# One more half-size product cut into quarters in each projection, and where its operand sums are placed

## The chip, the cores and the metric

The kernel runs on one core of a Trainium2 chip. The metric is device time in microseconds; the median of three runs is shown, and one further execution was taken by the hardware profiler. TensorE (PE) multiplies; VectorE (DVE) and ScalarE (ACT) read its results out of PSUM; GpSimd (POOL) adds and subtracts in SBUF; SyncE (SP) issues the DMAs.

## The reference

Two layers over 64 batches of 256 tokens by 512 features, all float32:

```python
# layer 0
h = relu(layernorm(x))
x = x + (adj @ h) @ W0 + b0
# layer 1: attention with 8 heads of 64, masked by adj
h = relu(layernorm(x))
q, k, v = (h @ Wq + bq), (h @ Wk + bk), (h @ Wv + bv)
attn = softmax(q @ k.T / 8 + (1 - adj) * -1e9)      # per batch and head
x = x + (attn @ v) @ Wo + bo
```

The projections q, k, v and o (512 features to 512 features) are what the change touches.

## The kernel before

**Groups and stages.** Two batches make a group, so there are 32 groups. Layer 0 fills the first 650 us or so and leaves its results in DRAM. The attention stage then works group by group; each group has two attention halves (`qd` 0 and 1, four heads each). From group `FIRST2 = 2` on, a cycle of the stage is: `attend(g, 0)` (denominators `pden` and the product with v, `pav`), `score(g, 1)`, then the query and key projections of group g+1 in the order `QK`, then `attend(g, 1)`, `score(g+1, 0)`, then the value projection of group g+1 interleaved with the output projection of group g in the order `VO`. The last group uses the orders `V1`, `O1` and `OL` instead.

**Seven products for eight.** A projection multiplies a 2 by 2 arrangement of weight blocks by a 2 by 2 arrangement of activation blocks, with seven products in the manner of Strassen and Winograd. The names are in `BLOCKS`: A is a11 b11, B is s3 t3, C is a12 b21, D is a22 t4, E is s4 b22, F is s2 t2, G is s1 t1. The `s` are sums of weight blocks, made once; the `t` are differences of activation blocks, made for each group (class `Halves`): t1 = b12 - b11, t3 = b22 - b12 (written over b12), t2 = b22 - t1, t4 = b21 - t2. One such product at full size is four matmuls of 128x128 by 256 columns (`product`).

**Quarter size.** `SMALL` names the products that are cut once more in the same way: seven matmuls of 128x128 by 128 columns in place of four of 256. They need the same seven combinations one level down: weight sums from `block_sums` (once, early in the stage) and activation sums from `Blocks.sums` (each group, on POOL), called by `block_hidden` for q, k and v and by `block_outputs` for o. Before, q, k and v have C to G at quarter size and o has C, D and E; A and B (and o's F and G) are at full size.

**How a quarter-size product gets out of PSUM.** `sums` multiplies the first four of the seven into a small bank: a running total and, beside it, a rest. Between two multiplications the total is read out. In `added` (C, D, E) ACT or DVE put these parts into the result; in `staged` (F, G) ACT copies them to SBUF, DVE adds the rest and later adds everything into the bank. The last three multiplications go straight into a bank (`last_three`).

**The order of work.** `QK`, `VO`, `V1`, `O1` and `OL` are written-out orders. In the token `qGf`, q is the projection, G the product, f its step; `kp00`, `qm11` and the like put or add a bank into one quarter of the result; `x` takes the next exponent (`next_exponent`, an ACT instruction at L1122); `|` is one tick of a clock. Work put down with `after(n, ...)` is issued n ticks later. Every engine works through what was issued to it in that order.

**POOL's queue around this.** In the value half: the inversion of the denominators (`invert`, L1163 to L1165: one multiply, one scale, one multiply, after an ACT logarithm and exponential), the subtraction of the row maximum for two of the score's four parts (L1108, the other two are done by DVE alone), the sums of the output operand (`t_o`, L481, and `block_outputs`, L578 to L580), the key sums (`key_sum`, L1129, four additions that `pden` needs), the hidden sums of the next group (`t_h`). In the query-key half: the rest of the hidden sums and `block_hidden`, then the inversion, the two subtractions, one sum of `t_o`, the key sums. `score` seeds two pairs of banks on ACT first and then runs what waits in the list `behind_seeds`, which is the inversion; after that come the score's matmuls and their evacuation.

**Buffers.** Denominators and their inverse (`den`, `rden`) lie in a tile called `rest`, which also holds the o sums of C and E. Key sums lie in the tile `as`, one buffer, rewritten in every half. Quarter-size sums of q, k and v lie in a tile `t2` and in a part of `spare`, those of o's D in `t24o`. Spare room for weight sums and these is taken from tiles of layer 0 that are no longer in use.

Of the kernel before, what the change touches and what calls it, by code (L numbers as in the profile page):

```python
# [8 lines left out]
F32 = mybir.dt.float32  # L9
# [48 lines left out]
def general_path(tc, x, adj, w0, b0, wq, bq, wk, bk, wv, bv, wo, bo, out):  # L58
# [154 lines left out]
V1 = (
    "vFa vA0 vFb vA1 vFc vFd x vA2 | vA3 vGa vFe vEa vp00 vCa vFf vGb | vB0 vEb vFg vCb vFi x vGc vFh vFj vFk vGd "
    "vFl | vEc vGe vEd vCc vEe vCd vp10 vGf vEf2 vDa vCe vGg vB1 vCf | vEf vDb vB2 x vGh vGi vGj vEg vGl vB3 | "
    "vCg vp11 vDc vCh vDd vGk x vDe vCi vDf vCj vDi vm11 | vDj vDk vCk vm10 vDg vEi vEj vCl vEk | vDh vEl0 vEl1 "
    "vEl2 vEh ")
# [11 lines left out]
def kernel(  # L229
# [314 lines left out]
    SMALL = {"q": "CDEFG", "k": "CDEFG", "v": "CDEFG", "o": "CDE"}  # L544
# [3 lines left out]
    def block_sums(n):  # L548

        todo = []  # L550
        for x in SMALL[n]:
            w = W[n][BLOCKS[x][0]]
            def part(i, j):
                return w[:, j, i * P:(i + 1) * P]
            s1, s2, s4 = (spare.pop(0) for _ in range(3))
            W2[n, x] = dict(a11=part(0, 0), a12=part(0, 1), a22=part(1, 1), s1=s1, s2=s2, s3=part(1, 0), s4=s4)
            eng = nc.vector if x in "FG" else nc.gpsimd
            for o, p, q, op in ((s1, part(1, 0), part(1, 1), ALU.add), (s2, s1, part(0, 0), ALU.subtract),
                                (part(1, 0), part(0, 0), part(1, 0), ALU.subtract), (s4, part(0, 1), s2, ALU.subtract)):
                todo.append((eng.tensor_tensor, o, p, q, op))  # L560
        return todo

    class Blocks:
# [7 lines left out]
        def operand(self, n):  # L571
            if n[0] == "t":
                return self.t[..., {"t1": 0, "t3": 1, "t2": 2, "t4": 3}[n], :]
            return self.x[..., int(n[1]) - 1, int(n[2]) - 1, :]

        def sums(self, eng):
            t, op = self.t, ALU.subtract
            eng.tensor_tensor(t[..., 0:2, :], self.x[..., :, 1, :], self.x[..., 0, :, :], op=op)  # L578
            eng.tensor_tensor(t[..., 2, :], self.operand("b22"), t[..., 0, :], op=op)
            eng.tensor_tensor(t[..., 3, :], self.operand("b21"), t[..., 2, :], op=op)  # L580

    def quartered(g, n, halves, blocks, by_token, place, first, seeds=None, multiplied=None, done=None):
# [102 lines left out]

        def added(x, to, quadrant=None, begin=False):
# [36 lines left out]
        product("B", "pc", True)  # L723
# [346 lines left out]
    A, AS, behind_seeds, exponents = {}, {}, [], []  # L1070

    def score(g, qd, sum_delay=5, exps=(3, 4, 5, 8)):
# [10 lines left out]
        for c in range(2):  # L1083
            for b in range(GB):
# [46 lines left out]
    def attend(g, qd):  # L1131
# [19 lines left out]
        if i == 0:  # L1151
            AS["rest"] = act.tile([P, 4, GN], F32, tag="yT1", name="rest")
        den, rden = AS["rest"][:, 0, :], AS["rest"][:, 1, :]
# [16 lines left out]
        else:  # L1170
            behind_seeds.append(invert)
# [98 lines left out]
    for g in range(NG):  # L1270
# [106 lines left out]
```

## Time and profile before

| what | us |
|---|---|
| median of 3 runs | 2641.59 |
| lowest and highest run | 2637.54, 2641.89 |
| profiled execution: its own time | 2640.46 |
| profiled execution: span from first to last instruction | 2638.1 |
| layer 0, before the first `pden` | 660.0 |
| one cycle of the steady stretch (two halves) | 62.0 |

The profile is of one execution. A group of instructions is given by line, engine, operation, names of what it writes and reads, shapes and count; then its busy time in us, the mean ns of one, and the idle time of its engine just before it. A float32 matmul shows as two records. A timeline line gives the start and the length in us; x2 or x4 at its end says that so many equal records were merged. The names in lines of the trace are the program's: `q_pc` is q's bank pc, `k_Fs` the small bank of k's product F.

### The profile page before, as it was taken

What the parts mean: (1) busy time and instruction counts of PE and PEld (TensorE: products, weight loads), DVE (VectorE), ACT (ScalarE), POOL (GpSimd) and SP (SyncE); (2) the same over time, 40 slices, a digit from 0 to 9 for tenths busy, and PEclk for the clock granted to TensorE, in tenths of its full rate; (3) what the DMA queues carried; (4) which work ended last, traced back from release to release, by engine and by line L of the source; (5) the groups of instructions that cost most, each with busy time, mean ns of one, the idle gap of its engine ahead of it and who ended that gap; (6) DMA issues with size and microseconds to landing.
All of it is one profiled execution on the core that took longest, in us unless ns stands there. A gap on an engine that the chain in (4) does not pass through costs nothing. (4 is left out here: it accounts for less than half of the span.)

```text
span 2638.1 us, 54578 instructions
## 1 busy us (share of the span) xinstructions
PE 2599.2 (99%) x21156; PEld 2291.1 (87%) x21156; DVE 1835.3 (70%) x3999; ACT 1292.5 (49%) x2742; POOL 1948.3 (74%) x1897
## 2 busy tenths in 40 slices
PE   7999999999999999999999999999999999999997
PEld 6999899998788888888888888888888888888886
DVE  5878788875466666666666666666666666666666
ACT  3444454543444545555555455544454555555542
POOL 5888887773777777777777777777777777777774
PEclk9999999999999999999999999999999999999999
DMA  5776667664111222111111111111122221111101
GB/s 131 200 197 183 173 166 184 166 167 100 33 49 49 64 62 66 52 49 49 49 49 49 49 49 49 49 49 49 49 65 63 61 56 49 49 49 49 49 33 49
DMA packets 281077, 211.20 MB, mean 80 GB/s; under 512 B 145904, under 2 KB 212976, under 8 KB 280816
## 3 DMA queue, kind: packets, MB, share of 16 engines
q1 hardware_dynamic: 280352, 207.15, 30.0%
q8 instruction: 169, 2.77, 0.4%
q14 instruction: 92, 0.75, 0.1%
q10 hardware_dynamic: 464, 0.52, 0.1%
HBM read 106.96 MB, written 100.66 MB: 79 GB/s over the span
## 5 line engine op out<-in xcount | busy, mean ns | idle before, releaser
L1163 POOL TENSOR_TENSOR rest<-rest 128x512 f32<-128x512 f32 x63 | 80.2, 1273 | 425.0 <-ACT rest L1162 425.0
L1098 DVE SCALAR_TENSOR_TENSOR a<-sc,top 128x512 f32<-128x512 f32 x256 | 159.0, 683 | 278.0 <-PE sc L1090 277.9
L1108 POOL TENSOR_TENSOR a<-a,top 128x1024 f32<-128x1024 f32 x125 | 293.2, 2369 | 47.5 <-DVE a L1101 47.5
L1129 POOL TENSOR_TENSOR as<-a 128x512 f32<-128x512 f32 x256 | 318.3, 1275 | 5.8 <-ACT a L1122 5.8
L1122 ACT ACTIVATE a<-a 128x1024 f32<-128x1024 f32 x256 | 271.8, 1063 | 0.6 <-POOL a L1108 0.5
L1090 PE MATMUL sc<-q,k 64*128 64x256 f32 x2048 | 240.0, 383 | 1.4 <-ACT sc L289 1.4
L1090 PEld LDWEIGHTS sc<-q,k 64*128 64x128 f32 x2048 | 196.6, 186 | 45.5 <-ACT rest L1161 25.5
L1145 PE MATMUL pav<-a,v 128*32 128x256 f32 x4096 | 235.0, 381 | 0.0
L1145 PEld LDWEIGHTS pav<-a,v 128*32 128x32 f32 x4096 | 133.8, 111 | 89.2 <-issue 2.0
L1154 ACT ACTIVATE rest<-pden 128x512 f32<-128x512 f32 x64 | 38.2, 597 | 340.7 <-PE pden L1138 340.7
L42 DVE BATCH_NORM_STATS2 st<-x 128x6 f32<-128x512 f32 x256 | 173.1, 676 | 8.8 <-DMA x<-in_x_dram 6.6
L1101 DVE SCALAR_TENSOR_TENSOR a<-sc,maskT 128x512 f32<-128x512 f32 x256 | 158.1, 678 | 0.0
L289 ACT ACTIVATE sc<-maskT 128x512 f32<-128x512 f32 x256 | 137.5, 591 | 0.0
L800 ACT ACTIVATE h<-x,nb,rs 128x512 f32<-128x512 f32 x128 | 93.9, 803 | 75.3 <-POOL nb L54 75.3
L927 ACT ACTIVATE h<-x,nb,rs 128x512 f32<-128x512 f32 x128 | 97.2, 808 | 52.0 <-POOL nb L54 47.1
L645 PE MATMUL o_pa<-wo_s,t_o 128*128 128x256 f32 x480 | 118.8, 380 | 0.0
L772 DVE TENSOR_TENSOR x<-o_pa,x 128x512 f32<-128x512 f32 x120 | 82.5, 687 | 50.4 <-PE o_pa L645 50.4
L1183 DVE TENSOR_TENSOR oT<-pav,rest 128x512 f32<-128x512 f32 x128 | 82.0, 681 | 29.3 <-POOL rest L1165 29.3
L1016 ACT ACTIVATE k<-k_pa,bk_c 128x256 f32<-128x256 f32 (+1 forms) x150 | 61.3, 449 | 78.4 <-PE k_pa L631 78.1
L861 POOL TENSOR_TENSOR hs<-h 128x512 f32<-128x512 f32 x31 | 39.3, 1269 | 73.8 <-ACT h L800 63.7
L645 PEld LDWEIGHTS o_pa<-wo_s,t_o 128*128 128x128 f32 x480 | 84.3, 191 | 7.8
L1030 ACT COPY v<-v_pa 128x512 f32<-128x512 f32 (+1 forms) x90 | 42.8, 475 | 97.2 <-PE v_pa L631 95.6
(1644 smaller groups left out, 8238.7 us busy)
## 6 DMA issues: line engine op xcount, KB each, us to landing
x<-in_x_dram SPq DMA_DIRECT2D x256, 128.0 KB, 3.1
residual<-x SPq DMA_DIRECT2D x256, 128.0 KB, 2.5
hidden<-r SPq DMA_DIRECT2D x128, 256.0 KB, 4.5
h1T<-hidden SPq DMA_DIRECT2D x64, 512.0 KB, 7.4
x<-residual SPq DMA_DIRECT2D x32, 1024.0 KB, 7.5
out_dram<-x SPq DMA_DIRECT2D x62, 512.0 KB, 4.1
w_sb<-in_L_gnn_weight_dram SPq DMA_DIRECT2D x1, 1024.0 KB, 9.5
wq_sb<-in_L_gnn_Wq_dram SPq DMA_DIRECT2D x1, 1024.0 KB, 8.2
```

Source lines behind the costliest of these rows:

```text
L42: nc.vector.bn_stats(st, src)
L289: nc.scalar.mul(t, seed, times)
L645: nc.tensor.matmul(t[:, m, :], lhs, rhs, start=starts, stop=True, skip_group_check=True)
L800: nc.scalar.activation(H0[g][:, t, :], xt[:, t, :], AF.Relu, bias=nb[:, t % n:t % n + 1], scale=rs[:, t % n:t % n + 1])
L927: nc.scalar.activation(h1[:, k * NT + t, :], xt[:, k * NT + t, :], AF.Relu, bias=nb[:, t:t + 1], scale=rs[:, t:t + 1])
L1090: nc.tensor.matmul(ps[j][:, kt * N:(kt + 1) * N], k[j * HD:(j + 1) * HD, c, kt * P:(kt + 1) * P], q[j * HD:(j + 1) * HD, c, :], start=(kt ...
L1098: nc.vector.scalar_tensor_tensor(o, ps[j].rearrange("p (k n) -> p k n", k=NT), SCALE, top_b[:, 0:NT, :], op0=ALU.mult, op1=ALU.subtract)
L1101: nc.vector.scalar_tensor_tensor(o.rearrange("p k n -> p (k n)"), ps[j], SCALE, maskT_f, op0=ALU.mult, op1=ALU.add)
L1108: nc.gpsimd.tensor_tensor(a, a, top_b, op=ALU.subtract)
L1122: nc.scalar.activation(a, a, AF.Exp)
L1129: nc.gpsimd.tensor_tensor(AS[c, b], a4[:, :, 0, :], a4[:, :, 1, :], op=ALU.add)
L1145: nc.tensor.matmul(po[f][h * 32:(h + 1) * 32, b * N:(b + 1) * N], v[:, k, h * HD + f * 32:h * HD + f * 32 + 32], A[h // 2, b][:, (h % 2) * ...
```

## The change

1. `SMALL` gets B (s3 t3) for q, k and v, and F (s2 t2) for o. B's first four multiplications are a new function, `chain`: ACT copies the running total straight into bank pc (steps c, e, g), the rest goes to SBUF (n) and DVE adds it into pc at the end (k). The block sums of B's weights are put on DVE.
2. `Blocks.sums` makes four separate subtractions, with t3 written over b12, so a set of sums takes three blocks of room and not four.
3. `block_hidden` keeps only the sums of t1, t2 and t4's blocks (D, F, G) at its old place. The sums of b21's blocks (C) go to `behind_seeds`, after the inversion, which is put first in that list. The sums of t3's blocks (B, new) and of b22's (E) go to a new list, `behind_scores`, that `score` runs when it is through.
4. `block_outputs` makes the sums of t2's and t4's blocks first, then those of b21 and b22.
5. `den` and `rden` lie in the first half of the key sums' tile `as`; the room of `rest`, `t2` and `t24o` becomes fixed tiles for the sums (`KEPT`) and spare blocks.
6. All five orders are written anew.

The core of the diff (of the orders, QK in full and most of VO):

```diff
 QK = (
-    "kFa kCi kFb kCj kCk qFa kFc qFb kFd x qB0 | qGa qFc qFd kFe qA0 qFe x qA1 | qFf kFf qA2 qFg kFg qA3 qFh | "
-    "kA0 kFh qp000 kA1 qp001 kDa kA2 x qFl kA3 | qCi qGb qCj kp000 qCk qFi kp001 qCl qFj qFk | qGc kFl qp100 qGd "
-    "qDa qp101 kCl kB0 qGe kB1 qDb x qGi | qGf kFi qGg kCa kFj kCb kFk qGh qGj kp100 qGk | kCc kp101 qGl kCd kGa "
-    "qDc kCe kGb qDd kCf kGi kGc qDe | qDf kGd kCg kDb kGe kB2 kCh kGf kDc kGg qDg | kB3 qDh kDd kGh kp110 qCa "
-    "kDe qEa kp111 kDf qB1 qEb qCb qB2 | kGl kDi kDj kDk kDg km10 qEc qEd | qCc kDh qEe qCd kEa qEf qCe qB3 qCf "
-    "kEb kGj qEf2 qp110 kGk | kEc qp111 km11 kEd qEg kEe qCg qm11 qDi kEf qDj qDk qCh | kEi kEf2 kEj qm10 qEi qEj "
-    "kEg qEk kEk qEl1 | qEl2 kEl0 kEl1 qEl0 kEh qEh kEl2 ")
+    "qFa kA0 qFb kA1 kFa qFc x qCa | kA2 kA3 kFb qGa kp000 qFd kFc | kp001 kFd qA0 qFe kFe qA1 x qFf kFf | qA2 "
+    "qFg kFg qA3 qFh kFi kFh qp000 kFj kFk qp001 | qCi kFl qCj x kCa qCk qCb qFi kCb qFj qCl qGb qCc kp100 qCd | "
+    "qFl kCc kp101 kCd kGa x qCe qGc kCe qGd kCf kGi qCf kGj | qGe kGk kGb qFk kCg qp100 qGf kCh kGc qp101 qCg "
+    "kGd | qGg qCh kBa kGe kBb qGh qGi kBc qGj kGf qGl qDa kGg kBd | qBa qDb kBe qBb kGh kBn qGk qBc qDc kGl qDd "
+    "kBf qDe qBd | qDf kBg kCi kCj qBn kCk qBe kBh kCl kBi qDg qBf | qDh qEa qBg kEa kBj qEb kDa kEb kBk qBh qBi "
+    "kDb qBj kp110 | kEc qBk kp111 qEc qEd kDc qp110 km11 kDd qp111 kDi kEd kDe qEf | kDj kDf kEf kDk qm11 kEi "
+    "qEe kEj kEe qDi qEf2 kEk km10 kDg kEl0 | qEi kEf2 qDj kDh qDk qEg kEl1 qEj qm10 qEk kEg qEl0 | kEl2 kEh qEh "
+    "qEl1 qEl2 ")
 VO = (
...
-    "vEb vGi vGh x vGj vEc vGl vEd vDc vEe vDd | vEf vDj vDe vDk vDf vGk oA0 vm10 oA1 vm11 | vDg oA2 vEf2 vDh oA3 "
-    "vEi op00 vEj vEk | vEg vEl0 oCi oCa vEh oF0 oCb oF1 vEl1 vEl2 | oF2 oF3 oCc op10 oCd oEa oDa | oCe oB1 oCf "
-    "oB2 oDb oEb oB3 oDc | op11 oDd oEc oEd oDe oG0 oDf oDi oEe oG1 oEf | oG2 oG3 oCg om11 oDj oDk | oDg oCh oCj "
...
+    "vA0 oAz vA1 oBz vA2 vA3 x | vFa vCi vCj vCk vFb vp00 vBa vBb vFc x | vFd vGa vCl vFi vFj vFe vFk vBc vCa vGb "
+    "vFf | vCb vBd vFg vGc vGd vBe vCc vFh vGe vCd vFl x oA0 oEa | vCe vGf vCf vBf vp10 oEb oA1 vGg vCg vBn oA2 "
+    "vGh vBg | oA3 vCh x vGl oB0 vBh op00 oFa vBi | oFb vBj vDa vBk vEa vGi vDb vEb vGj vp11 vGk vEc | vDc vm11 "
+    "vEd vDd vEe vDi vEf vDe vDj vDf vDk vEi vEf2 vEj | vm10 vEk vDg vEl0 vEg vDh oFc oFd vEl1 oFi vEh oFe oFj | "
+    "vEl2 oFk oDa oFf oCa oFg oB1 oCb oB2 oFh | oFl oEc oEd oCc op10 oCd oB3 oCe oCi | oCf oCj op11 oG0 oG1 oDb "
+    "oEe oG2 oEf | oG3 oDc om11 oDd oCg oDi oDe oDj oDf | oDk oEi oCh oCk om10 oDg oEj oEk oDh oEg oCl0 | oEh "
+    "oCl1 oEl ")
...
-    SMALL = {"q": "CDEFG", "k": "CDEFG", "v": "CDEFG", "o": "CDE"}
+    SMALL = {"q": "BCDEFG", "k": "BCDEFG", "v": "BCDEFG", "o": "CDEF"}
...
-            eng = nc.vector if x in "FG" else nc.gpsimd
+            eng = nc.vector if x in "BFG" else nc.gpsimd
...
         def operand(self, n):
+            if n == "t3":
+                n = "b12"
             if n[0] == "t":
-                return self.t[..., {"t1": 0, "t3": 1, "t2": 2, "t4": 3}[n], :]
+                return self.t[..., {"t1": 0, "t2": 1, "t4": 2}[n], :]
             return self.x[..., int(n[1]) - 1, int(n[2]) - 1, :]
 
         def sums(self, eng):
-            t, op = self.t, ALU.subtract
-            eng.tensor_tensor(t[..., 0:2, :], self.x[..., :, 1, :], self.x[..., 0, :, :], op=op)
-            eng.tensor_tensor(t[..., 2, :], self.operand("b22"), t[..., 0, :], op=op)
-            eng.tensor_tensor(t[..., 3, :], self.operand("b21"), t[..., 2, :], op=op)
+            for o, p, q in (("t1", "b12", "b11"), ("t3", "b22", "b12"), ("t2", "b22", "t1"), ("t4", "b21", "t2")):
+                eng.tensor_tensor(self.operand(o), self.operand(p), self.operand(q), op=ALU.subtract)
...
+        def chain(x, b):
+
+            t, total, rest = sums(x, "adbf")
+            held = {}
+
+            def copy(name, i, k):
+                def todo():
+                    o = part(take(b, full=True), i, k)
+                    nc.scalar.copy(o, like(o, total()))
+                step(x + name, todo, t, b)
+
+            def keep_rest():
+                held[0] = act.tile([P, 2, 2, P], F32, tag="stage", name=f"{n}_{g}_{x}", bufs=2)[:, 0, 0:1, :]
+                nc.scalar.copy(held[0], rest())
+
+            def add_rest():
+                o = part(banks[b], 1, None)
+                add(o, o, like(o, held[0]))
+            copy("c", 0, 0)
+            step(x + "n", keep_rest, t)
+            copy("e", 1, 0)
+            copy("g", None, 1)
+            last_three(x, "hij", b)
+            step(x + "k", add_rest, b)
+
...
-        product("B", "pc", True)
+        if "B" in SMALL[n]:
+            chain("B", "pc")
+        else:
+            product("B", "pc", True)
...
-    kept = []
+    KEPT = {}
 
     def block_hidden(g, step):
 
-        t = act.tile([P, GB, 4, P], F32, tag="t2", name=f"t2_{g}")
-        both = Blocks(H1T[g][:, :, 2:4, :].rearrange("p k c (n j) -> p k c n j", j=P), t)
-        last = Blocks(HH[g].all.rearrange("p t c (n j) -> p t c n j", j=P), kept[0])
-        after(step, both.sums, nc.gpsimd)
+        x = H1T[g]
+        both = Blocks(x[:, :, 2:4, :].rearrange("p k c (n j) -> p k c n j", j=P), KEPT["h2"])
+        third = Blocks(x[:, 1, 0:2, :].rearrange("p c (n j) -> p c n j", j=P), KEPT["h3"][:, 3])
+        last = Blocks(HH[g].all.rearrange("p t c (n j) -> p t c n j", j=P), KEPT["h3"][:, 0:3])
         after(step, last.sums, nc.gpsimd)
-        H2[g] = {"C": both.one(0), "E": both.one(1), "G": last.one(0), "F": last.one(1), "D": last.one(2)}
+        behind_seeds.append(lambda: both.one(0).sums(nc.gpsimd))
+        behind_scores.append(lambda: third.sums(nc.gpsimd))
+        behind_scores.append(lambda: both.one(1).sums(nc.gpsimd))
+        H2[g] = {"C": both.one(0), "E": both.one(1), "G": last.one(0), "F": last.one(1), "D": last.one(2), "B": third}
 
     def block_outputs(g, step):
         x = OT[g][:, 2:4, :].rearrange("p c (k n j) -> p k c n j", k=GB, j=P)
-        if g < NG - 1:
-            t4 = act.tile([P, 4, P], F32, tag="t24o", name=f"t24o_{g}")
-            t = AS["rest"][:, 2:4, :].rearrange("p k (q j) -> p k q j", j=P)
-        else:
-            t4 = kept[0][:, 0]
-            t = act.tile([P, GB, 4, P], F32, tag="t2", name=f"t2o_{g}")
-        both = Blocks(x, t)
-        last = Blocks(HO[g].t["t4"].rearrange("p c (n j) -> p c n j", j=P), t4)
+        t = KEPT["o" if g < NG - 1 else "h3"]
+        both = Blocks(x, t[:, 0:2])
+        last = Blocks(HO[g].all[:, 1:3].rearrange("p t c (n j) -> p t c n j", j=P), t[:, 2:4])
         if g == NG - 1:
             both.sums(nc.vector)
             last.sums(nc.gpsimd)
         else:
+            after(step, last.sums, nc.gpsimd)
             after(step, both.sums, nc.gpsimd)
-            after(step, last.sums, nc.gpsimd)
-        O2[g] = {"C": both.one(0), "E": both.one(1), "D": last}
+        O2[g] = {"C": both.one(0), "E": both.one(1), "F": last.one(0), "D": last.one(1)}
...
+        while behind_scores:
+            behind_scores.pop(0)()
...
-        if i == 0:
-            AS["rest"] = act.tile([P, 4, GN], F32, tag="yT1", name="rest")
-        den, rden = AS["rest"][:, 0, :], AS["rest"][:, 1, :]
+        den, rden = (AS["all"][:, 0, b].rearrange("p j n -> p (j n)") for b in range(GB))
...
-            behind_seeds.append(invert)
+            behind_seeds.insert(0, invert)
...
                 t = pool.tile([P, n, P], F32, tag=tag, name=f"spare_{len(spare)}")
-                spare.extend(t[:, i, :] for i in range(n if tag != "x3" else 4))
-            kept.append(t[:, 4:].rearrange("p (t q) j -> p t q j", q=4))
+                first = 0
+                if used:
+                    first = 3 * used[1]
+                    KEPT[used[0]] = t[:, 0:first].rearrange("p (t q) j -> p t q j", q=3)
+                spare.extend(t[:, i, :] for i in range(first, n))
```

More of the change, by code (lines that the diff above doesn't have):

```diff
@@ L204 @@
-    "kEb kGj qEf2 qp110 kGk | kEc qp111 km11 kEd qEg kEe qCg qm11 qDi kEf qDj qDk qCh | kEi kEf2 kEj qm10 qEi qEj "
-    "kEg qEk kEk qEl1 | qEl2 kEl0 kEl1 qEl0 kEh qEh kEl2 ")
-VO = (
-    "vA0 oAz vA1 oBz vA2 vA3 x | vFa vB0 vB1 vp00 vCa vFb vB2 x | vDa vCb vFc vGa vFd vGb vB3 vFe vCc | vp11 vCd "
-    "vFf vCe vFi vCf vFg vFj vFk x vDi vFh vCg vFl | vGc vGd vCi vCh vGe vCj vp10 vCk vGf vCl vEa vGg | oB0 vDb "
-    "vEb vGi vGh x vGj vEc vGl vEd vDc vEe vDd | vEf vDj vDe vDk vDf vGk oA0 vm10 oA1 vm11 | vDg oA2 vEf2 vDh oA3 "
-    "vEi op00 vEj vEk | vEg vEl0 oCi oCa vEh oF0 oCb oF1 vEl1 vEl2 | oF2 oF3 oCc op10 oCd oEa oDa | oCe oB1 oCf "
-    "oB2 oDb oEb oB3 oDc | op11 oDd oEc oEd oDe oG0 oDf oDi oEe oG1 oEf | oG2 oG3 oCg om11 oDj oDk | oDg oCh oCj "
-    "oCk oDh oEi om10 oEj oEk oEg oCl0 | oEh oCl1 oEl ")
+    "qFa kA0 qFb kA1 kFa qFc x qCa | kA2 kA3 kFb qGa kp000 qFd kFc | kp001 kFd qA0 qFe kFe qA1 x qFf kFf | qA2 "
@@ L213 @@
 V1 = (
[L214 to L217, printed above, removed]
+    "vFa vA0 vFb vA1 vFc vFd x vA2 | vA3 vGa vFe vBa vp00 vBb vFf vGb | vCa vBc vFi vFg vCb vGc x vBd vFh vFj vCc "
+    "vFl vEa | vBe vGd vEb vCd vGe vBf vCe vEc vCf vBn vGf vBg vEd vFk vGg | vCg vEe vBh vGh vp10 vBi vEf2 vBj x "
@@ L218 @@
+    "vCh vCi vDa vBk vGi | vDb vGj vp11 vGk vCj vGl vCk vEf x vDc vDd vm11 vDi | vDj vEg vDe vDk vDf vEi vCl vEj "
+    "vEk vm10 vDg vEl0 | vEh vEl1 vDh vEl2 ")
 O1 = (
-    "oCi oBz oCj oCk oB0 oAz oB1 x oA0 | oA1 oDa oEa oA2 x | oA3 oEb oCa op00 oB2 oEc oCb oEd oCl0 oF0 | oF1 oEe "
-    "oEf oF2 oCl1 x oF3 oCc | op10 oCd oB3 oCe oEg oDb oG0 op11 oG1 | oEh x oG2 oCf oG3 oDi om11 oDc oDd | oCg "
-    "oDe oDj oDf oDk oEi oCh oEj om10 oEk oDg | oEl oDh ")
+    "oAz oCi oCj oCk oA0 oBz oA1 x oFa | oB0 oCa oFb oA2 oFc x oA3 | oFd op00 oB1 oFe oEa oCl0 oFf oFi oFg oFj | "
@@ L222 @@
+    "oEb oFk oCb oB2 oFh oFl oCc x oB3 op10 oEc | oEd oDa op11 oCd oG0 oCe oDb oG1 oCf oG2 | oEe x oEf oDc oG3 "
+    "oCl1 oDi om11 oDj oDd | oCg oDe oEg oDf oDk oEi oCh oEj om10 oEk oDg | oEl oDh oEh ")
 OL = (
-    "oAz oBz oA0 oA1 oB0 | oA2 oA3 oB1 oB2 op00 | oCa oEa oCb oB3 oEb oF0 op11 oCc oCd | oEc oCe oEd oCf oF1 oEe "
-    "oF2 oEf oF3 | oDa op10 oCi oCj oCk oDb oEg oCl0 oG0 oDc | oCl1 oDd oEh oG1 oDe oCg oDf oG2 oCh oG3 | oDg "
-    "om11 oDi oDj oDk oDh oEi om10 oEj oEk | oEl ")
+    "oAz oBz oA0 oA1 oA2 | oA3 oB0 oB1 oFa op00 | oCi oFb oCa oCj oCb oCk oFc oCl0 oFd oEa oFe oCc | oCl1 oCd oEb "
@@ L228 @@
+    "oFf oCe oFi oCf oFg oFj oFk oEc oFh oCg oFl oEd | oDa oB2 op10 oB3 oDb oEe oG0 oCh oDc | op11 oDd oG1 oDe "
+    "oG2 oDf oEf oG3 oDg | om11 oDi oDj oDk oDh oEg oEi om10 oEj oEk oEh | oEl ")
 @with_exitstack
@@ L1068, in quartered_outputs @@
         return quartered(g, "o", halves, O2.pop(g), True, place, None, {"pa": row[:, :HF], "pc": row[:, HF:]}, done=done)
-    A, AS, behind_seeds, exponents = {}, {}, [], []
+    A, AS, behind_seeds, behind_scores, exponents = {}, {}, [], [], []
     def score(g, qd, sum_delay=5, exps=(3, 4, 5, 8)):
@@ L1280 @@
         if g == 0:
-            for pool, n, tag in ((const, 4 * DC, "w0_sb"), (const, 4, "w0_s1"), (const, 4, "w0_s2"), (const, 4, "w0_s4"),
-                                 (const, 4, "adjT"), (const, 4, "b0_r"), (tmp, 4, "u"), (tmp, 4, "u"), (tmp, 4, "u"),
-                                 (act, 4, "t24"), (xpool, 4 * DC, "x3")):
-                t = pool.tile([P, n, P], F32, tag=tag, name=f"spare_{len(spare)}")
-                spare.extend(t[:, i, :] for i in range(n if tag != "x3" else 4))
-            kept.append(t[:, 4:].rearrange("p (t q) j -> p t q j", q=4))
+            for pool, n, tag, used in ((const, 4 * DC, "w0_sb", None), (const, 4, "w0_s1", None), (const, 4, "w0_s2", None),
+                                       (const, 4, "w0_s4", None), (const, 4, "adjT", None), (const, 4, "b0_r", None),
+                                       (tmp, 4, "u", None), (tmp, 4, "u", None), (tmp, 4, "u", None), (act, 4, "t24", None),
+                                       (act, 4, "t24o", None), (xpool, 16, "x3", ("h3", 4)), (act, 8, "t2", ("h2", 2)),
+                                       (act, 16, "yT1", ("o", 4))):
+                t = pool.tile([P, n, P], F32, tag=tag, name=f"spare_{len(spare)}")
+                first = 0
[3 more added lines that the diff above has]
+                spare.extend(t[:, i, :] for i in range(first, n))
         for n, at in (("q", 7), ("k", 16)) if g == 0 else (("v", 2),) if g == 1 else (("o", 2),) if g == 2 else ():
```

## The prediction

> **What bounds the kernel now.** I read the page first, then one cycle of the steady stretch: two attention halves (pden to pden), which repeat from about 800 to 2560 us.
>
> ```profile
> PE 2599.2 (99%) x21156; PEld 2291.1 (87%) x21156; DVE 1835.3 (70%) x3999; ACT 1292.5 (49%) x2742; POOL 1948.3 (74%) x1897
> ...
> PEclk9999999999999999999999999999999999999999
> ...
> 1477.40:1539.40 62.00, 62.00 (x559) 54.52 (x558) 42.44 (x98) 31.67 (x73) 46.21 (x39) 1.00 0.19 52
> ```
>
> TensorE has work in all 62.0 us of the cycle (columns: PE, weight load, DVE, ACT, POOL) at full clock; POOL has 15.8 us idle, ACT 30.3. A busy PE need not be a PE that issues back to back, so I looked at starts. Next, the groups of the product that is replaced, and one quarter-size group:
>
> ```profile
> L645 PE MATMUL q_pc<-h1T,wq_sb 128*128 128x256 f32 x240 | 66.7, 380 | 0.0
> ...
> L631 PE MATMUL q_Es<-t,spare 128*128 128x128 f32 x120 | 23.2, 275 | 0.0
> ...
> 1501.24 1.03 PE L645 MATMUL q_pc<-h1T,wq_sb 128*128 128x256 f32 x4
> 1502.11 0.38 PE L631 MATMUL k_pc<-t_h,wk_sb 128*128 128x128 f32 x2
> ...
> 1503.22 0.39 PE L631 MATMUL q_Es<-t,wq_s 128*128 128x128 f32 x2
> 1503.44 0.39 PE L631 MATMUL q_Cs<-t,spare 128*128 128x128 f32 x2
> ```
>
> A product is two records. Starts are 0.87 us apart over four 256-wide records and 0.22 over two 128-wide ones; over the steady stretch the spacings are 0.216 and 0.112 us a record. The means of 380 and 275 ns overlap each other and are no price. Gaps above these spacings come to only about 0.3 us a cycle. So what leaves PE's list leaves the time, if no other engine becomes late. POOL is the one to check, in the timeline:
>
> ```profile
> 1485.63 1.27 POOL L1163 TENSOR_TENSOR rest<-rest 128x512 f32<-128x512 f32 x1
> ...
> 1488.92 4.69 POOL L1108 TENSOR_TENSOR a<-a,top 128x1024 f32<-128x1024 f32 x2
> ...
> 1491.35 1.05 ACT L1122 ACTIVATE a<-a 128x1024 f32<-128x1024 f32 x1
> ...
> 1526.17 1.27 POOL L578 TENSOR_TENSOR rest<-oT 128x512 f32<-128x512 f32 x1
> ...
> 1530.77 4.95 POOL L1129 TENSOR_TENSOR as<-a 128x512 f32<-128x512 f32 x4
> ```
>
> POOL runs without a gap from 1517.7 to the end of the next query-key half's key sums (in the cycle shown, 1499.8). The reader is to see that the first exponent of POOL's pair starts at 1491.35, just behind POOL's first subtraction (1488.92 + 2.37): that chain is already tight.
>
> [...]
>
> **The change, part by part.**
>
> 1. PE. By the two instruction lists, 480 full-size products go and 840 quarter-size ones come: four for seven, in 4 blocks (q, k, v: s3 t3; o: s2 t2) of 30 groups, 120 times. Each is 8 x 0.216 - 14 x 0.112 = 0.16 us; 120 x 0.16 = **19.2 us off**, all on PE, 0.64 a cycle. Added waits on PE's instructions cost nothing before: 128-wide records with and without a wait both come at 0.112.
>
> 2. ACT and DVE, a cycle. A chain has three 128-wide copies and a 256-wide one (3 x 265 + 365 ns = 1.16) and one DVE add (415); three of them, and for o's s2 t2 two copies, one wide one, and adds of 415 and 690. ACT +4.4 us on 31.7, DVE +2.35 on 42.4: hidden under 62 us of PE, if in time. The chain's steps (product, copy, product) stand at least 0.89 us of PE work apart; the shortest such step before, in k's s1 t1 block, is 0.66 and shows no gap.
>
> 3. POOL, a cycle. Hidden sums were 1286+736+733 and 1812+1001+1001 ns, 6.6 us; now four of 1000 and twelve of 457, 9.5. Output sums were 4.4 us; now eight of 730, 5.8. Together +4.4 on 46.2. Costless as a sum, so I follow the queue.
>  - Output sums in the value half take 6.0 instead of 4.6 us: key sums (L1129) start at 1532.3 instead of 1530.8, end at 1537.2. PE reaches pden 0.33 earlier, at 1539.1: 1.9 us left. Of o's quarter products, oFc comes 13.7 us of PE work into this half (about 1530.1), its t2 block by 1528.5; oEc at 1532.8, its block by 1531.6.
>  - Then in the clock of 1477: hidden sums of full size end at 1480.8 (five microseconds of work, PE 0.33 nearer), three-in-one block sums at 1484.9 (first needed at 1486.8), the inversion at 1488.2, where it ended at 1488.9: DVE's divide comes earlier, as 2.8 us of block sums went behind it. Then b21's block, 1.9 us, to 1490.1; the two subtractions to **1492.4 and 1494.8, where they were done at 1491.3 and 1493.6**. What was moved behind them: b12's block until 1496.7 (t3 by 1495.8, kBb wants it at 1497.0), b22's until 1498.6, t1 of o, key sums by about 1504.7 against pden at 1507.9.
>  - ACT takes the exponents in its own order. By durations it is free for the fourth at about 1494.1 and now waits until 1494.8; exponent (next start 0.96 later), then the copy qGe (0.27): 1496.1. PE comes to qGf, which needs it, at 10.4 us of its list, 1496.0. With the signal's way this is **0.2 us late a cycle, or nothing**; estimates good to some 0.3. I take 0.1 x 29 = 3 us, ends 0 and 0.5 x 29 = 14.5.
>
> 4. Denominators in the key sums' tile. No instruction added; ACT writes after pden's products have read it, as before. New: the next key sums may only be written after the divide. Divides end by 1490.3 and about 1518.1; the key sums follow at 1494.8 and 1530.8 even before. Free; it costs only if divides slip 4 us. The tiles taken from it hold block sums; readers of the last round end before POOL returns to them.
>
> 5. Weights: 16 more block sums on DVE, once (about 0.4 us each at most), between products whose operands are due a dozen steps later: nothing. No DMA is added or moved; SP's queue is as it was.
>
> 6. The end. The value half of the last group is short and PE waits there for key sums (3.0 and 2.0 us at 2582 and 2585): they come 1.5 later, and its 0.16 of gain is lost. After the last divide, o's order does quarter products before it needs late sums; before, PE idled 1.7 and 1.7 us there. I put the end at +0.5, from -1 to +2.
>
> Sum: the profiled execution has 2640.46 us beside its span of 2638.1; 2640.5 - 19.2 + 3 + 0.5 = 2624.8. The median shown is 1.1 above the profiled execution, the lowest run 2.9 below; I take **2624.5**.
>
> **The rivals.**
> - Gain in full (no late copy): 2621.5. For it: the subtractions are late by less than what my durations are good for. Against it: the item above.
> - Much of it eaten: 0.4 to 0.5 us a cycle at qGf or at pden, 2633 to 2636. The tight chain at 1491.35 speaks for it; the 1.9 us before pden against.
> - **Slower**: ACT blocked behind the fourth exponent. In-order ACT then also holds the evacuations qp100 and qp101, and PE loses nearly what POOL is late. It decides from 0.65 us a cycle of PE loss, that is subtractions some 0.45 us later than worked out; at 1.0 us later PE loses 1.2 x 29 = 35 us, and the time is 2657. What POOL's rows show of equal forms (730, 457, repeated within some ns) speaks against so large an error; new strided forms speak for a little.
> - The change doesn't do what it says: quarter-size records limited by weight loads (192 ns each). Then seven would cost 14 x 0.19 and the kernel lose about 110 us; the 0.112 spacing rules it out.
>
> **How the numbers follow.** What a measurement here can tell from no change is 0.2%, 5.3 us. Chances: the forecast with a small late copy or none, 0.78; much eaten but still clearly faster, 0.09; within 0.2%, 0.05; slower 0.08. The range goes from 2617.5 (all the gain, end better by 1, a low execution) to 2636 (0.45 us a cycle lost).
>
> **What would show it.** Right: L645 rows of q_pc, k_pc and v_pc gone, o_pa of wo_s halved, 128-wide spacing 0.112, cycle 61.4 to 61.6 where it was 62.0; pden-to-pden of the value half 30.85 or less. The fourth exponent at POOL's heels shows step 3; a regular gap at q_Gs behind an ACT copy shows its price. Wrong: PE waiting at pden for key sums in each cycle, or a cycle above 62.

## The result and the profile after

| what | before | after |
|---|---|---|
| median, us (8 runs each, one chip) | 2641.05 | 2632.84 |
| lowest and highest | 2637.54, 2641.89 | 2631.73, 2634.63 |
| span of the profiled execution | 2638.1 | 2630.2 |

The ratio is 0.9972 (95% interval 0.9961 to 0.9983): faster, but by 8 us (0.3%) where 17 were forecast. Below stand the page's first line, its row of granted TensorE clock, and the waits of ACT and POOL around the scores (engine and line, what it waited for, us in total, times, longest):

```profile
PE 2588.6 (98%) x21876; PEld 2301.6 (88%) x21876; DVE 1909.8 (73%) x4166; ACT 1379.4 (52%) x3192; POOL 2075.6 (79%) x2256
...
PEclk9999999999999999999999999999999999999998
```

```profile
POOL as L1191 <- ACT as L1190: 278.9, 34, 8.9
...
ACT a L1152 <- POOL a L1136: 15.3, 55, 0.4
```

The lines of the kernel have moved: exponent L1122 is now L1152, subtractions L1108 are L1136, key sums L1129 are L1159, block sums L578 are L582, inversion L1163 is L1191, DVE's additions are L802. The last line, exponents waiting for POOL's subtraction, came to 0.5 us in all before; now 55 exponents wait 0.28 us each. POOL's own wait for the inversion, the first line, fell from 425.0 us to 278.9: POOL has more to do. Next a steady cycle, in the timeline:

```profile
1473.77 1.07 PE L1168 MATMUL pden<-as,ones 128*32 128x256 f32 x16
...
1504.52 1.07 PE L1168 MATMUL pden<-as,ones 128*32 128x256 f32 x16
...
1535.38 1.07 PE L1168 MATMUL pden<-as,ones 128*32 128x256 f32 x16
```

```profile
1486.50 4.69 POOL L1136 TENSOR_TENSOR a<-a,top 128x1024 f32<-128x1024 f32 x2
...
1491.23 1.06 ACT L1152 ACTIVATE a<-a 128x1024 f32<-128x1024 f32 x1 [0.36 <-POOL a L1136]
...
1492.14 0.39 PE L633 MATMUL k_Cs<-spare,spare 128*128 128x128 f32 x2
1492.19 0.25 ACT L670 COPY q_G<-q_Gs 128x128 f32<-128x128 f32 x1
...
1492.49 0.30 PEld L633 LDWEIGHTS q_Gs<-spare,spare 128*128 128x128 f32 x2 [0.15 <-ACT q_G L670]
1492.49 0.49 PE L633 MATMUL q_Gs<-spare,spare 128*128 128x128 f32 x2
```

The cycle is 61.61 us where it was 62.0. POOL's second subtraction ends at 1491.19 (1486.50 + 4.69), and the fourth exponent of the query-key half starts at its heels. The copy of q_G comes behind it on ACT, at 1492.19, in the order issued. PE is due at q_Gs at 1492.36 (1492.14 and two records of 0.112) but starts at 1492.49, and its second record comes another 0.10 late. The same gap stands at that place in 27 of the 28 steady cycles and sums to 6.1 us.

Interval by interval, from one `pden` to the next (a half of a cycle), in the two profiled executions:

| part of the span | before | after | change | forecast |
|---|---|---|---|---|
| up to the first `pden` | 659.97 | 659.44 | -0.5 | 0 |
| five intervals from there (to the second `pden` of group 2) | 165.53 | 167.40 | +1.9 | -0.8 |
| 28 steady cycles | 1737.3 | 1725.1 | -12.1 | -14.9 |
| last two intervals | 46.76 | 47.77 | +1.0 | 0.0 for this row and the next together |
| last `pden` to the end | 28.56 | 30.43 | +1.9 | (in the row above) |

The forecast's column spreads its 19.2 us by where the 120 blocks lie (17.9 steady, 0.8 start, 0.5 end), then adds its +3 to the steady cycles and its +0.5 to the end. The start misses by 2.7 us, the steady cycles by 2.8, the end by 2.9. The second of the five intervals at the start is 36.63 us in both traces; it holds a stretch in which TensorE runs at half pace (granted clock 0.50 for 3.41 us), and in traces without that stretch it is 34.94 (see the last section). Within a cycle, a value half went from 31.18 to 30.85, a query-key half only from 30.85 to 30.76, where the shorter list gives 0.32 each.

### The profile page after: what moved, and what is told of

Same layout as the page of the kernel before. It is cut to its first block, busy times and chain, and to the rows that moved or that the text cites. A ratio compares the mean times of both kernels' runs of the same rounds, so it can differ in the third digit from the quotient of the medians.

```text
span 2630.2 us, 57376 instructions
## 1 busy us (share of the span) xinstructions
PE 2588.6 (98%) x21876; PEld 2301.6 (88%) x21876; DVE 1909.8 (73%) x4166; ACT 1379.4 (52%) x3192; POOL 2075.6 (79%) x2256
## 3 DMA queue, kind: packets, MB, share of 16 engines
q8 instruction: 175, 2.87, 0.4%
## 5 line engine op out<-in xcount | busy, mean ns | idle before, releaser
L1136 POOL TENSOR_TENSOR a<-a,top 128x1024 f32<-128x1024 f32 x125 | 293.5, 2369 | 40.3 <-DVE a L1129 40.3
L1159 POOL TENSOR_TENSOR as<-a 128x512 f32<-128x512 f32 x256 | 318.3, 1276 | 5.8 <-ACT a L1152 5.8
L1191 POOL TENSOR_TENSOR as<-as 128x512 f32<-128x512 f32 x63 | 80.2, 1273 | 284.3 <-ACT as L1190 278.9
L1152 ACT ACTIVATE a<-a 128x1024 f32<-128x1024 f32 x256 | 271.7, 1063 | 15.3 <-POOL a L1136 15.3
L1182 ACT ACTIVATE as<-pden 128x512 f32<-128x512 f32 x64 | 38.3, 599 | 294.6 <-PE pden L1168 294.6
L1129 DVE SCALAR_TENSOR_TENSOR a<-sc,maskT 128x512 f32<-128x512 f32 x256 | 158.4, 681 | 0.0
L483 POOL TENSOR_TENSOR t_o<-oT,t_o 128x512 f32<-128x512 f32 x63 | 80.5, 1279 | 12.1 <-DVE t_o L483 9.6
L1211 DVE TENSOR_TENSOR oT<-pav,as 128x512 f32<-128x512 f32 x128 | 82.1, 683 | 8.4 <-POOL as L1193 8.4
L582 POOL TENSOR_TENSOR spare<-h1T,spare 128x128 f32<-128x128 f32 x180 | 82.4, 458 | 7.1
L1044 ACT ACTIVATE q<-q_pa,bq_c 128x256 f32<-128x256 f32 (+1 forms) x150 | 61.8, 456 | 48.9 <-PE q_pa L633 36.6
L802 DVE TENSOR_TENSOR x<-o_pa,x 128x512 f32<-128x512 f32 x120 | 82.4, 687 | 6.1 <-PE o_pa L647 4.8
L52 POOL TENSOR_TENSOR rs<-rs,mhalf 128x2 f32<-128x2 f32 (+1 forms) x97 | 80.0, 825 | 8.1
```

The costliest lines, as they stand in the source:

```text
L582: eng.tensor_tensor(self.operand(o), self.operand(p), self.operand(q), op=ALU.subtract)
L1129: nc.vector.scalar_tensor_tensor(o.rearrange("p k n -> p (k n)"), ps[j], SCALE, maskT_f, op0=ALU.mult, op1=ALU.add)
L1136: nc.gpsimd.tensor_tensor(a, a, top_b, op=ALU.subtract)
L1152: nc.scalar.activation(a, a, AF.Exp)
L1159: nc.gpsimd.tensor_tensor(AS[c, b], a4[:, :, 0, :], a4[:, :, 1, :], op=ALU.add)
```

## The experiments

Each time below is a median, given against the median of the kernel before, which was run beside it on the same chip. The experiments ran on three chips (1 to 3 and the three edits of 4 together on one, the rest of 4 and 5 to 7 on the second, the combined run of 5 and 8 on the third), so ratios compare between them and medians less well. The changed kernel's own ratio is 0.9972.

The theory after the result: the shortening of PE's list is there in full, and is given back in three places: at q_Gs behind the fourth exponent (6.1 us), at the start behind DVE's weight sums, and at the end behind DVE's block sums. Rivals: the exponent's place is only where another lateness shows, or the quarter-size chains themselves cost more than their spacing.

**1. The fourth exponent later.** The token `x` moves from before `qCe qGc` to after `kBc` in `QK`:

```diff
-    "... kGa x qCe qGc ... qGi kBc qGj kGf ..."
+    "... kGa qCe qGc ... qGi kBc x qGj kGf ..."
```

> The changed kernel with one token of QK moved: the fourth exponent goes from ahead of qCe to behind kBc, 3.1 us of PE work later, when POOL's second subtraction (it ends 9.3 us into the query-key half) is long done. Theory (ACT's queue waits 0.36 us for POOL there and holds the copy that qGf needs): the 0.23 us gap before and in q_Gs goes, the query-key half falls from 30.76 to 30.53 us, about 27 x 0.23 = 6 us off the 2632.8 of the changed kernel: 2626.7. Rival (POOL's lateness is general and comes out elsewhere): a gap of like size appears at another product, the half stays at 30.7 or more, and the time at 2632 to 2633.

Measured 2626.58 us against 2638.72 (ratio 0.9954, 0.9941 to 0.9968). The query-key half is 30.53, the gap at q_Gs is gone, and 27 steady cycles are 5.9 us shorter than after the change. Its waits:

```profile
ACT q_G L670 <- PE q_Gs L633: 19.9, 31, 0.9
...
ACT a L1152 <- POOL a L1136: 1.6, 10, 0.2
```

ACT now waits for PE at that copy, not PE for ACT. So the copy behind the exponent was the whole of the steady loss: 30.53 + 30.85 is 0.65 less than before's 62.03. That is all that the shorter list gives, and the quarter-size chains cost nothing beyond their spacing.

**2. The last group's block sums one step later.** DVE's sums of b21 and b22 for the last output projection are issued a tick later:

```diff
-            both.sums(nc.vector)
+            after(1, both.sums, nc.vector)
```

> The changed kernel with the last group's DVE sums of b21 and b22 issued one tick later, behind the evacuations that PE waits for. Theory (t3 of the quarter blocks, now written over b12, makes DVE wait 1.2 us for POOL's full-size t4, and the four evacuations of o stand behind it): the gap of 3.9 us at o_pb near 2610 shrinks to 1 us or less, a later one of up to 1 us may come where C and E need these sums; 2 to 3.5 us off, 2629.5 to 2631. Rival (the order OL asks for late sums by itself): the gap only moves, less than 1 us off.

Measured 2629.50 against 2638.72 (0.9964, 0.9951 to 0.9977); the times alone don't part it from the changed kernel. Last `pden` to end fell from 30.43 to 29.41 in the two traces. In the six other traces whose end is not edited it is 30.42 to 31.81, so the gain is 1.0 to 2.4 us, where 2 to 3.5 was expected. The timeline of PE, after the change first, then with the edit:

```profile
2613.83 0.79 PE L633 MATMUL o_pb<-wo_sb,oT 128*128 128x128 f32 x2 [3.76 <-DVE x L802]
```

```profile
2613.80 0.79 PE L633 MATMUL o_pb<-wo_sb,spare 128*128 128x128 f32 x2 [2.25 <-DVE spare L582]
```

The 3.76 us wait for an evacuation that stood behind the sums is gone, but PE comes soon to a product that needs the sums themselves, and waits 2.25 there. The theory is half right, and so is the rival: part of the wait only moved.

**3. The weight sums moved.** v's go to group 0, and the sums of o's F, the new ones, come eight ticks later:

```diff
-        for n, at in (("q", 7), ("k", 16)) if g == 0 else (("v", 2),) if g == 1 else (("o", 2),) if g == 2 else ():
+        for n, at in (("q", 7), ("k", 16), ("v", 23)) if g == 0 else (("o", 2),) if g == 2 else ():
...
-                after(at + i // 4, *work)
+                after(at + i // 4 + (8 if n == "o" and i >= 12 else 0), *work)
```

> The changed kernel with the weight block sums of v made in group 0 behind the last product that reads them at full size, and the four DVE sums of o's F eight ticks later. Theory (DVE's sums with two SBUF operands stand still while POOL's long subtraction runs, 1.35 and 2.32 us where 0.28 is usual, and hold the evacuations): the intervals between pden starts of groups 1 and 2, 34.09 and 31.71 us, fall to about 32.5 and 30.8; 2 to 2.5 us off, 2630.5. Rival (the start is slow from the order QK in its first use): no more than 0.5 us off.

Measured 2630.09 against 2638.72 (0.9967, 0.9955 to 0.9979); again the times alone don't part it from the changed kernel, the intervals do. The third interval went from 34.09 to 30.53, below the 32.76 of before, where v's sums of F and G had stood in the same place. The fifth stayed, 31.71 to 31.76. So v's sums were the loss of the third, and eight ticks did not help o's. Nor is v's new place free: there the sums take 1.2 to 1.35 us each beside POOL's key sums, DVE's additions wait behind them, and PE waits 1.80 us at 723.63. The second interval is 37.01, where experiment 1's trace, also without a half-pace stretch there, has 34.94.

What the loss is made of is seen in the timeline after the change, in that third interval:

```profile
739.11 4.72 POOL L1136 TENSOR_TENSOR a<-a,top 128x1024 f32<-128x1024 f32 x2
...
740.26 1.35 DVE L312 TENSOR_TENSOR spare<-wv_sb 128x128 f32<-128x128 f32 x1
741.65 2.32 DVE L312 TENSOR_TENSOR spare<-spare,wv_sb 128x128 f32<-128x128 f32 x1
...
744.36 0.28 DVE L312 TENSOR_TENSOR spare<-wv_sb,spare 128x128 f32<-128x128 f32 x1
...
745.03 0.49 PE L633 MATMUL q_pb<-h1T,wq_sb 128*128 128x128 f32 x2 [1.73 <-DVE q_F L802]
```

A DVE sum of 0.28 us takes 1.35 and 2.32 beside POOL's two subtractions (2.36 each): each ends 0.1 to 0.2 us after one of POOL's (741.5 and 743.8). DVE's addition to q_F, behind them in its queue, is late, and PE waits 1.73 for it.

**4. Sums of o's F on POOL**, with the three edits above together. First those three alone:

> The three edits of this call together. Theory (three separate losses, at the fourth exponent, at the end and at the start): they add up, 6 + 2.5 + 2.3 = about 11 us off 2632.8, 2622, which is 19 us below the kernel before: what TensorE's shorter list is worth. Rival (matmuls of quarter size cost more than 0.112 us a record, or waits come back elsewhere): 2627 or more.

Measured 2623.01 against 2638.72 (0.9941, 0.9927 to 0.9954): query-key half 30.53, fifth interval 31.78, last `pden` to end 29.58. The gains add up, interval by interval. Then:

```diff
-            eng = nc.vector if x in "BFG" else nc.gpsimd
+            eng = nc.vector if x in "BFG" and n != "o" else nc.gpsimd
```

> All three edits of the earlier call, with the weight sums of o's F now on POOL (behind the key sums of the same half) and not on DVE. Theory (any DVE sum with two SBUF operands in the query-key half of group 2 holds the evacuations, wherever it stands): the interval of that half, 31.71 in the changed kernel and 31.78 with the sums eight ticks later on DVE, falls to 30.6 or so, 1.1 us less than with the three edits alone. Rival (the half is slow because it is the first with o's products behind it): 31.7 stays.

Measured 2623.47 against 2641.19 (0.9931, 0.9917 to 0.9945); the fifth interval is 30.53, all of its loss gone. Against the three edits alone the median doesn't tell 1.2 us; the interval does.

**5. v's s3 t3 back at full size**, which takes the change away in the value half alone (and four of DVE's weight sums at the start). v's s3 t3 then reads a t3 of which the quarter block sums have overwritten a part: the values of that block are changed, its work isn't.

```diff
-    SMALL = {"q": "BCDEFG", "k": "BCDEFG", "v": "BCDEFG", "o": "CDEF"}
+    SMALL = {"q": "BCDEFG", "k": "BCDEFG", "v": "CDEFG", "o": "CDEF"}
...
-    "... vp00 vBa vBb vFc ... vBd ... vBf ..."      # VO; V1 in the same way
+    "... vp00 vB0 vB1 vFc ... vB2 ... vB3 ..."      # the other steps of vB are dropped
```

> The changed kernel with v's s3 t3 back at full size (four products of 256 columns for seven of 128, no chain; the other three blocks stay at quarter size). Theory (a block cut to quarters is worth 8 x 0.216 - 14 x 0.112 = 0.16 us of TensorE's list, and the value half has no late wait): the value half goes from 30.85 to 31.01 us, 30 x 0.16 = 4.8 us more than the changed kernel. Rival (the quarter-size chain costs as much as it saves, the gain came from elsewhere in the new orders): 30.85 stays, no more than 1 us.

Measured 2634.64 against 2641.19 (0.9976, 0.9966 to 0.9986). The value half grew from 30.85 to 31.02, as it should, but the query-key half fell from 30.76 to 30.59: 27 steady cycles are the same to 0.01 us. My theory had the half right and the total wrong. The reason I then formed: POOL works without a break from its subtractions in the value half's score through to those in the next query-key half, so each 0.17 us that PE saves between those two places brings it 0.17 earlier to q_Gs, where it waits. The test is the same edit with the late exponent out of the way (edits 1 and 5 together):

> The fourth exponent placed later, as in the first experiment, and v's s3 t3 left at full size, with part of t3 overwritten by the quarter block sums (that block's values are changed, its work is the one of full size). Theory (what v's quarter blocks save in the value half is real, 0.16 us, and came back in the query-key half only because POOL's subtractions stand behind that half's score and PE then reached q_Gs earlier than the exponent; with the fourth exponent out of the way nothing gives it back): value half 31.02, query-key half 30.53, steady sum larger than the first experiment's 1657.6 by 27 x 0.17 = 4.6 us, span about 2628.5. Rival (v's quarter blocks are worth nothing in any placement, since another chain anchors the cycle): query-key half falls below 30.53 by 0.17 again, and the span is that of the first experiment, 2624.

Measured 2630.13 against 2639.37 (0.9964, 0.9950 to 0.9978): value half 31.02, query-key half 30.56 (30.53 in experiment 1), steady cycles 5.0 us longer than there. So v's quarter is worth its 0.17 us a cycle, once nothing downstream is late.

**6. The subtractions later still**, the price of the slower rival: two more of POOL's block subtractions (some 0.46 us each) stand ahead of the subtractions.

```diff
+        c = both.one(0)
+        for _ in range(2):
+            behind_seeds.append(lambda: nc.gpsimd.tensor_tensor(c.operand("t4"), c.operand("b21"), c.operand("t2"), op=ALU.subtract))
```

> The changed kernel with two more POOL subtractions (128x128, a repeat of a sum that is there) ahead of the score's two subtractions, which makes these some 0.9 us later in each query-key half. Theory (ACT waits in order behind the fourth exponent, so PE loses at qGf what POOL is late): the gap there grows from 0.23 to about 1.1 us, the half from 30.76 to 31.6 to 31.7, 27 x 0.9 = 24 us more than the changed kernel: about 2656, slower than before. Rival (the 0.23 us is a fixed cost of the copy and PE, other work takes up lateness): under 8 us more.

Measured 2665.74 against 2641.19 (1.0093, 1.0077 to 1.0108). The query-key half grew by 1.06 us, 27 steady cycles by 28.7.

Its waits (lines stand three further down here):

```profile
ACT a L1155 <- POOL a L1139: 45.1, 56, 1.3
...
PEld q_Gs L633 <- ACT q_G L670: 23.5, 56, 0.5
```

About 0.92 us more on POOL is 1.06 more on PE: the lateness is passed on whole.

**7. The late sums not put behind the score**, but where the other sums of the group are:

```diff
-        behind_seeds.append(lambda: both.one(0).sums(nc.gpsimd))
-        behind_scores.append(lambda: third.sums(nc.gpsimd))
-        behind_scores.append(lambda: both.one(1).sums(nc.gpsimd))
+        for late in (both.one(0), third, both.one(1)):
+            after(step, late.sums, nc.gpsimd)
```

> The changed kernel with the block sums of b21, t3 and b22 made at their old place, right behind those of t1, t2 and t4, ahead of the inversion. Theory (POOL's queue: twelve subtractions of 0.46 us, 5.7 us, stand ahead of the inversion, which then ends near 1490.3 where it ends at 1484.6, and ahead of the two subtractions, which end at 1495 where they end at 1491.2): DVE sits 5 to 6 us before its divide, ACT 3 to 4 us before the exponents, and PE loses 3 to 4 us a cycle, 2720 to 2750. Rival (the deferral is a convenience; the evacuations wait for nothing): within 15 us of the changed kernel.

One run: 2795.41 us against 2641.19, span 2793.6. The query-key half is 35.6 to 37.2, on average 5.5 more, beyond the 3 to 4 expected.

```profile
DVE oT L1210 <- POOL as L1192: 166.4, 28, 6.0
...
ACT a L1151 <- POOL a L1135: 119.4, 56, 3.9
...
PE q_pb L633 <- DVE q_F L802: 100.0, 29, 3.5
```

(Lines stand one higher here.) DVE waits 5.9 us before each divide, as expected; its addition to q_F stands behind the divide, and PE waits some 3.5 for that addition in each cycle, within the 3 to 4. The rest comes after the wait: in each cycle TensorE then runs at half pace for 3.41 us or twice that (last section), which the expectation left out. Without the new place for the late sums the kernel is 154 us slower than before.

**8. The order of o's products at the end refilled**, on top of experiment 4: B2, B3 and Ea come ahead of the first product that needs DVE's block sums.

```diff
-    "... oA3 oB0 oB1 oFa op00 | oCi oFb oCa ... oFd oEa oFe ... oDa oB2 op10 oB3 oDb ..."
+    "... oA3 oB0 oB1 oB2 oB3 oFa op00 | oCi oFb oEa oCa ... oFd oFe ... oDa op10 oDb ..."
```

> The best version so far (fourth exponent later, weight sums moved and o's on POOL, the last block sums one step later), with the order of o's products at the end changed: B2, B3 and quarter block E a of o stand ahead of the first product that needs DVE's last block sums. Theory (the last gap is PE reaching that product before the block sums[...]): the gap of 2.25 us falls to 1.2 or less, no stretch of 0.43 us spacing follows, and last pden to end falls from 29.8 to 27.5 to 28.3; span 2619.5 to 2620.5. Rival (the work put ahead is only taken from later places, where PE then waits for late evacuations or late sums as long): a new gap of 1 us or more further on, last pden to end 29.3 to 30.

Measured 2621.32 against 2639.37 (0.9927, 0.9911 to 0.9944). Span 2620.4; last `pden` to end 28.8, between the theory's 27.5 to 28.3 and the rival's 29.3 to 30. The wait fell from 2.25 to 1.66 and a new one of 0.93 stands further on. What went whole is the half-pace stretch behind the wait: the granted clock is 1.00 from 2602 to 2611. That it would go was the author's estimate. PE's timeline, refilled:

```profile
2605.33 0.49 PE L633 MATMUL o_pb<-wo_sb,spare 128*128 128x128 f32 x2 [1.66 <-DVE spare L582]
2605.65 0.39 PE L633 MATMUL o_Fs<-spare,spare 128*128 128x128 f32 x2
2605.88 0.39 PE L633 MATMUL o_Fs<-wo_s,t_o 128*128 128x128 f32 x2
```

and the same place in the version with o's sums on POOL:

```profile
2605.60 0.80 PE L633 MATMUL o_pb<-wo_sb,spare 128*128 128x128 f32 x2 [2.25 <-DVE spare L582]
2606.19 0.63 PE L633 MATMUL o_Fs<-spare,spare 128*128 128x128 f32 x2
2606.61 0.63 PE L633 MATMUL o_Fs<-wo_s,t_o 128*128 128x128 f32 x2
```

Starts are 0.43 us apart where they are 0.22 above. This version and that of experiment 4 with o's sums on POOL are the fastest found, some 18 us below before, and beat both kernels; the intervals of their ratios don't part them.

## Why the prediction was right and wrong

- **Step 1, PE: right.** With experiment 1 the cycle is 61.38, 0.65 below before where 0.64 was worked out, and experiment 5 shows v's share by itself. The q_pc groups of L645 are gone and q_Bs records come at 0.112.
- **Step 2, ACT and DVE: right in what it concludes.** Nothing but the named exponent and copy is late in the steady cycle. DVE's busy time grew by 2.3 us a cycle, as worked out; ACT's by 2.9 (31.67 to 34.55) and not 4.4: the durations do add up to 4.6 more, but they overlap in the trace.
- **Step 3, POOL: the layout right, the last term mis-sized.** The second subtraction ends 9.30 us after the first product of the query list (1481.89 to 1491.19); the step had 9.3. Key sums of the value half end 1.85 us ahead of `pden`; it had 1.9. It then worked out 0.2 us late a cycle and took 0.1, because its errors were 0.3. The measured loss is 6.1 us in all, about 0.23 in each of 27 cycles, where 3 was taken. An estimate in the middle of its error is still the estimate; halving it toward zero was 3 us of the miss.
- **Step 4, denominators: right as far as the trace goes.** Key sums never wait for DVE's divide. The denominators in a tile of their own were not tried.
- **Step 5, weights: wrong.** "Nothing" should have been 2.7 us: the start grew by 1.9 us, with 1.3 in its third interval and 0.9 in its fifth, where it was to shrink by 0.8. The sums were priced at 0.4 each at most, by themselves, and their queue was taken as slack. One took 2.32 us, and what was named as consumer (products a dozen steps later) wasn't what waited: DVE's own next addition was. The sign stood in the trace of before, unread: its third interval was 32.76 where the steady one was 30.85, with the sums of F and G at that spot.
- **Step 6, the end: wrong.** The +1.5 at the short value half came, 22.52 to 24.02. "Before, PE idled 1.7 and 1.7 us there" was read as room; the second of these waits became 3.76. One part is a new wait of DVE. The in-place t3 may overwrite b12 only when those who read it are through, and POOL's last t4 sum reads the same tile:

```profile
2608.75 1.10 PE L647 MATMUL o_pc<-wo_sb,oT 128*128 128x256 f32 x4 [0.72 <-DVE oT L483]
...
2609.12 0.42 DVE L582 TENSOR_TENSOR spare<-oT 128x256 f32<-128x256 f32 x1
2609.28 1.38 POOL L483 TENSOR_TENSOR t_o<-oT,t_o 128x512 f32<-128x512 f32 x1 [9.64 <-DVE t_o L483]
...
2610.70 0.42 DVE L582 TENSOR_TENSOR oT<-oT 128x256 f32<-128x256 f32 x1 [1.16 <-POOL t_o L483]
2611.04 1.81 DVE L582 TENSOR_TENSOR spare<-oT,spare 128x256 f32<-128x256 f32 x2
...
2612.77 0.68 DVE L802 TENSOR_TENSOR x<-o_pa,x 128x512 f32<-128x512 f32 x1
```

  DVE waits 1.16 us, then its next two sums take 0.9 each beside POOL where the one before took 0.42, and every evacuation behind them is late. Four separate subtractions with one in place was noted as a saving of room; as a wait it was not costed. But before, DVE was not much quicker to its first evacuation:

```profile
2618.45 0.67 PE L645 MATMUL o_pc<-wo_sb,oT 128*128 128x256 f32 x2 [1.66 <-DVE oT L481]
...
2618.83 0.69 DVE L578 TENSOR_TENSOR t2o<-oT 128x512 f32<-128x512 f32 x1
...
2621.70 0.68 DVE L772 TENSOR_TENSOR x<-o_pa,x 128x512 f32<-128x512 f32 x1
...
2622.76 0.49 PE L631 MATMUL o_Es<-wo_s,oT 128*128 128x128 f32 x2 [1.69 <-DVE x L772]
```

  From the first of the sums to that evacuation it took 2.87 us before (2618.83 to 2621.70) and 3.65 after (2609.12 to 2612.77), 0.8 more. The other 1.3 us of the longer wait is PE's: the new order `OL` gives it 1.3 us of work between the two waits (2608.75 to 2610.07), where before had 2.6 (2618.45 to 2621.07). Behind the 3.76 us TensorE then runs at half pace until 2616.7, an estimated 1.4 us more (half of the 2.9 us from 2613.8 on). No run has t3 in a place of its own, so these shares are read from the traces and not shown by an experiment.
- **The rivals.** "Much of it eaten", 2633 to 2636, is nearly where the result fell, with its mechanism at about half its price and the rest from the start and the end. The slower rival was real but not near: some 0.92 us later than after the change, PE loses 0.23 + 1.06 = 1.29 a cycle (experiment 6) where 1.2 was worked out for 1.0; the kernel is then at 2665.7 and not at 2657, for the start and the end lose their part too. "Gain in full", 2621.5, is where the versions come out in which all three places are mended, 2623.5 and 2621.3. That quarter-size records would be limited by weight loads is ruled out by their spacing, still 0.112.

The three misses, 2.8, 2.7 and 2.9 us, less 0.5 in layer 0 (which no run explains), account for the 7.8 us between the forecast change of the span, -15.7, and the measured -7.9.

## What to carry to other kernels

Where the queue of an engine is tight, as ACT's was here behind the fourth exponent, what is saved on the bottleneck upstream of it is only paid out once the late instruction is moved (here 5.9 us over 27 cycles, experiment 1). Look for the queued instruction that stands in the way (here one exponent ahead of one copy) and put it behind. Price an added instruction beside the neighbours that it will run with (a sum of 0.28 us took 2.32 here), and name the next instruction of its own engine as the first that waits. Where a buffer is written in place, list who reads it, at the start and the end as well as in the steady loop. Where an order is written anew, look at what work it leaves for the bottleneck between two waits.

## What the hardware showed that was not expected

- **DVE's sums of two SBUF operands took longer beside POOL's work.** 0.28 us became 1.35 and 2.32, 0.42 became 0.9. In the third interval the DVE sums end 0.1 to 0.2 us after POOL's subtractions do. DVE's additions out of PSUM keep their 0.28 us beside the same POOL subtractions (at 1489.15 in the steady cycle). POOL's subtractions hardly changed (4.72 us for two against 4.69), but at the end its sums of 128x256 took 0.96 and 0.78 where 0.73 is usual.
- **After some waits TensorE runs at half pace, and after the same wait not always for the same time.** At the end of the kernel the same wait of 3.76 us stands in seven traces. After the change (below, with the next 3.4 us), and then in experiment 1 (window; us; busy PE, weight load, DVE, ACT, POOL; clock; DMA):

```profile
2613.30:2616.70 3.40, 2.87 (x13) 2.87 (x14) 2.80 (x10) 0.00 (x0) 0.86 (x2) 0.50 0.58 223
2616.70:2620.10 3.40, 3.40 (x27) 2.96 (x25) 2.72 (x6) 0.64 (x2) 0.00 (x0) 1.00 0.25 90
```

```profile
2605.20:2608.50 3.30, 2.26 (x10) 2.26 (x11) 2.83 (x10) 0.00 (x0) 1.36 (x2) 0.50 0.42 158
2608.50:2611.90 3.40, 3.40 (x18) 3.40 (x17) 1.91 (x6) 0.64 (x2) 0.00 (x0) 0.50 0.43 160
```

  The granted clock is 0.50 for 3.41 us in four of the seven and for twice that in three. Last `pden` to end is 30.4 to 30.7 in the four and 31.5 to 31.8 in the three, with no difference in the code there. At the start, a wait of 2.18 us is followed by half pace in seven of the twelve traces and not in five. Before, and then experiment 1:

```profile
715.11 3.59 PE L488 MATMUL o_0a<-wo_sb,oT 128*128 128x256 f32 x8 [2.18 <-ACT o_0a L289]
```

```profile
715.39 1.99 PE L490 MATMUL o_0a<-wo_sb,oT 128*128 128x256 f32 x8 [2.19 <-ACT o_0a L291]
```

  Before, the granted clock is 0.50 from 715.35 to 718.76, and the eight records take 3.59 us where experiment 1's take 1.99. In layer 0 it stayed at 1.00 behind a wait of 2.49 us (before, from 38 to 50). So the length of a wait alone doesn't settle whether half pace follows it, nor for how long; what does is not shown. The stretch in the second interval of the start cost an estimated 1.7 us (36.63 against the 34.94 of experiment 1).
